# A two-layer graph attention kernel: the turn of the layers with three PSUM tiles for the corrections, gathers chunk by chunk into kept tiles, three row buffers and another order

## The chip, the cores and the metric

The kernel runs on one core of one Trainium2 chip. The core has a matrix engine (PE, with its weight loads listed as PEld), a vector engine (DVE), a scalar engine (ACT), a GpSimd engine (POOL), a sync engine (SP) that issues most plain transfers, and 16 DMA engines. The metric is the device time of one execution in microseconds (us); the median of several runs counts.

## The reference, cut to what matters

A graph has N = 6250 nodes with 256 features and E = 200000 edges, sorted by destination. Two graph attention layers follow each other, the first with 4 heads of 64, the second with 1 head of 256.

```python
h = jnp.maximum(_layernorm(x, axis=-1), 0.0)
x = x + _L0_gnn_ref(h, edge_index, edge_attr_32, ...)

def _gat(x, src, dst, ea, Wg, a_s, a_d, Wge, a_e, b, n, h, f):
    hx = (x @ Wg).reshape(n, h, f)
    he = (ea @ Wge).reshape(-1, h, f)
    al = leaky_relu(einsum(hx, a_s)[src] + einsum(hx, a_d)[dst] + einsum(he, a_e), 0.2)
    m = segment_max(al, dst, num_segments=n)
    al = jnp.exp(al - m[dst])
    al = al / segment_sum(al, dst, num_segments=n)[dst]
    out = segment_sum(hx[src] * al[:, :, None], dst, num_segments=n)
    return out.reshape(n, h * f) + b
...
    te = relu(edge_attr @ We0 + be0) * exp(x @ Wo0 + bo0)[src][:, None]
    s2, d2, ea2 = _add_self_loops(src, dst, te, n)
    x = relu(_gat(x, s2, d2, ea2, Wg0, as0, ad0, Wge0, ae0, bg0, n, HEADS, PH) + x)
    te = relu(edge_attr @ We1 + be1) * exp(x @ Wo1 + bo1)[src][:, None]
    s2, d2, ea2 = _add_self_loops(src, dst, te, n)
    x = _gat(x, s2, d2, ea2, Wg1, as1, ad1, Wge1, ae1, bg1, n, 1, D) + x
    return x + orig
```

Each edge needs the row `hx[src]` of its source node: a gather of about 1 KB per edge. The second layer gathers rows of a table that the first layer makes, so the first layer's last nodes have to be finished before the second layer's gathered rows are all valid. This is the turn of the layers.

## The kernel before

**Tables and steps.** A table T[l] in DRAM holds one row per node for each layer: the features times the layer's weights and a few extra columns. The edges are cut into 1563 chunks of 128, and the chunks into 66 steps per layer: 64 steps of 24 chunks, one of 14, one of 13. Steps are counted through both layers, k = 0 to 131; steps 63, 64 and 65 are the last three of the first layer, step 66 is the first of the second.

**One step.** `gather` (L896 to L907) issues one indirect transfer per chunk from POOL: 128 rows of T[l] into `G[:, c, :]`, a tile of 128 partitions by 24 chunks by 270 columns. Then `logits` (its first reader of the gathered rows is L1158), `ends`, `links` and `maxima` work out the softmax weights with segmented scans on DVE; `scale` (DVE, L1266, first layer) or `scale_rows` (ACT, L1275, second layer) multiplies the rows by them; `onehots` (L1095) builds on DVE a matrix S that says which edge belongs to which of the step's up to 112 nodes; `sums` (L1285) multiplies S by G chunk by chunk on PE and adds up in one PSUM tile `u`; `evict` copies it to SBUF. `finish`, `rows1`, `rows2` and `rows3` turn the sums into node rows: in the first layer `nodes0` ends with two adds into a row buffer (L1370, L1372), `rows1` and `rows2` make the next layer's row on PE (L1378, L439), and `rows3` adds the bias (L443), takes one exponential (L1390) and stores the row to T[1] (L1419) and to a node buffer `nd` (L1421, L1424), all from SP. The edge terms of the next step are made by `rphase1`, `spread`, `parts`, `blocks`, `rphase2`, `adst` and `edge_rows` beside it.

**Buffers.** The G tiles come from three pools of one buffer each, step k from pool k modulo 3. A new tile from a pool can be written only when the tile before it in that pool is done with. `G0` is the tile of step 0, made in the prologue. There are two row buffers `trow1` (L431, L1368), used in turn. Each engine runs its instructions in the order in which the program issues them; nothing is reordered.

**The turn.** `ending` (L770) writes out by hand the order of steps 63 (`a`), 64 (`b`), 65 (`c`) and of step 66 (`after`). Step 66 gathers early, into step 63's tile, chunk by chunk in the order 0 to 23 (`gather(after, a["G"])`), before the last rows of T[1] are there; the last 256 rows of T[1] are filled with zeros beforehand (`lacking`). When the last nodes are done, the missing rows are put in by matrix products: `sources` (L1055) loads the source index of each of step 66's edges, spread over all partitions, into a scratch tile X from pool 2, the tile place of step 65 and later of step 68; `select` (L1063) makes two selector matrices on DVE (L1066), the first in a one-hot buffer, the second in X behind the source row; `lack_rows` (L1068) loads the last 256 rows of T[1] into two tiles; `complete` (L1075) does for each of the 24 chunks two products (L1083) into one of three PSUM regions and an eviction on DVE (L1084) that adds them to G. Two of the three regions are the halves of one PSUM tile `y`. The corrections are issued in three lots of eight with the edge terms of step 66 between them, and its one-hots ahead of the last lot.

After that the main loop goes on with step 66. Each turn of the loop begins with the gather of the next step: step 67's was the first to read the whole of T[1], step 68's goes to a new tile in place of the scratch.

Of the kernel before, what the change touches and what calls it, by code (L numbers as in the profile page):

```python
# [22 lines left out]
F32 = mybir.dt.float32  # L23
BF = mybir.dt.bfloat16
I32 = mybir.dt.int32
# [6 lines left out]
P = 128  # L32
# [47 lines left out]
class Kernel:  # L80
# [329 lines left out]
    def fixed_rows(self):  # L410
        nc, cp = self.nc, self.cp
        self.crow = cp.tile([1, D + self.L[0].H], F32, name="crow")
        self.cl = [cp.tile([36, P + 1], F32, name=f"cl{i}") for i in range(2)]
        for t in self.cl:
            nc.gpsimd.memset(t, -BIG)

        self.cnt = cp.tile([P, self.NS, 2], F32, name="cnt")
        self.mt = cp.tile([P, 4 * C + 4], F32, name="mt")
        x = 33 * C - 1
        fb = cp.tile([P, 8 * C + 2 * x], F32, name="fb2")  # L420
        self.fb = [fb[:, 8 * C * i:8 * C * i + 2 * x] for i in range(2)]
        for t in (self.mt, fb):
            nc.gpsimd.memset(t, 0.0)


        self.aq = [cp.tile([P, 4, 32], BF, name=f"aq{i}") for i in range(2)]
        for t in self.aq:
            nc.gpsimd.memset(t, 0.0)
        self.trow1 = []
        L1 = self.L[1]  # L430
        for i in range(2):  # L431
            self.trow1.append(cp.tile([P, L1.TW + D], F32, name=f"t1row{i}"))
        self.tw4 = cp.tile([P, 4, self.L[0].TW + D], F32, name="tw4")
        self.tws = [self.tw4[:, i, :] for i in range(4)]
# [153 lines left out]
    def index_load(self, g, pool):  # L588
        nc, ss = self.nc, self.groups[g]
        c = self.cs[ss[0]]  # L590
        o = sum(self.cs[:ss[0]])
        w = len(ss) * c
        di = pool.tile([P, 2, 4 * C], I32, name="gi", bufs=2)
        for i, n in enumerate(("dst", "dnx")):
            nc.sync.dma_start(di[:, i, :w], self.a[n][:, o:o + w])
        return di
# [50 lines left out]
    def edges(self, ctx):  # L647
        nc = self.nc
        self.gp += [self.pool(f"gath{i}", 1, ctx) for i in range(1, 3)]
        self.sp = self.pool("onehot", 2, ctx)  # L650
        self.wp = self.pool("work", 2, ctx)
        self.np_ = self.pool("nodes", 2, ctx)
        self.xp = self.pool("index", 1, ctx)
        self.ps_y = self.pool("ps_y", 1, ctx, space=PSUM)
        self.ps_1 = self.pool("ps_1", 1, ctx, space=PSUM)
        self.ps_f = self.pool("ps_f", 1, ctx, space=PSUM)
        self.lf = self.ps_1.tile([P, 512], F32, name="lf")
        nc.vector.memset(self.lf[0:4, 0:1], -BIG)
        steps = self.steps
        self.state = {0: None, 1: None}  # L660
        self.nodes(steps[0])
        self.gather(steps[0])
        if self.NS % 2:
            self.load_lb(1)
        self.spread(steps[0])
        self.parts(steps[0])
        self.blocks(steps[0])
        drain(self.rphase1(steps[0]))
        self.load_ea(1)
        self.rphase2(steps[0])  # L670
        self.adst(steps[0])
        self.onehots(steps[0])
        drain(self.soon)
        self.edge_rows(steps[0])

        pv = late = None
        self.ahead, self.rest = 1, None
        for k, st in enumerate(steps):
            nx = steps[k + 1] if k + 1 < len(steps) else None
            if st["s"] + 2 >= self.NS:  # L680
                continue
            for q in steps[k + 1:k + 3]:
                if q["L"] is st["L"] and "tw" not in q:
                    self.nodes(q)
            self.load_lb(k + 2)
            left = 99
            if self.ahead < len(self.groups):
                left = self.groups[self.ahead][0] - 2 - (self.ahead + 2 >= len(self.groups)) - k
            if self.rest is None and left <= 2:
                gi = self.index_load(self.ahead, self.xp)  # L690
                self.rest = self.index_group(self.ahead, self.xp, gi)
            if st["s"] + 3 == self.NS:
                self.ending(st, *steps[k + 1:k + 3], pv, late, steps[k + 3] if k + 3 < len(steps) else None)
                pv = late = None
                continue
            self.gather(nx)
            st["rows"] = st["L"].l
            drain(self.logits(st))
            self.ends(st)
            self.spread(nx)  # L700
            self.parts(nx)
            y = self.rphase1(nx)
            next(y)
            self.links(st)
            if late:
                self.rows2(late)
            self.load_fl(k + 1)
            self.blocks(nx)
            drain(self.maxima(st))
            drain(y)  # L710
            self.load_ea(k + 2)
            self.rphase2(nx)
            self.adst(nx)
            if "S" not in st:
                self.onehots(st)
            if st["rows"]:
                self.scale_rows(st)
            else:
                drain(self.scale(st))
            self.carried(st)  # L720
            self.sums(st)
            if late:
                self.rows3(late)
                late = None
            self.onehots(nx)
            if pv:
                drain(self.finish(pv))
            self.evict(st)
            if pv:
                self.rows1(pv)  # L730
                late = pv
            self.index_on(left)
            if k == 4 and self.early:
                self.lacking()
            if k >= 6:
                next(self.late, None)
                next(self.late, None)
            self.edge_rows(nx)
            if st["s"] + 4 == self.NS:
                drain(self.finish(st))  # L740
            pv = st
        self.flag()
# [9 lines left out]
    def ending(self, a, b, c, pv, late, after):  # L752
# [41 lines left out]
        self.sums(a, (n // 2, n))  # L794
        early = after and self.early
        if early:
            self.gather(after, a["G"])
        self.load_fl(k + 2)
        drain(self.maxima(b))
        self.evict(a)  # L800
# [59 lines left out]
        drain(f)  # L860
        self.rows1(c)
        self.rows2(c)
        self.rows3(c)
        if after:
            fill = iter(())
            if early:
                self.lack_rows(after)
                self.select(after)
                fill = self.complete(after)
            else:  # L870
                self.gather(after)
            self.nodes(after)
            self.spread(after)
            self.parts(after)
            self.blocks(after)
            for _ in range(C // 3):
                next(fill, None)
            self.rphase2(after)
            self.adst(after)
            for _ in range(C // 3):  # L880
                next(fill, None)
            self.edge_rows(after)
            self.onehots(after)
            drain(fill)

    def flag(self):
        nc = self.nc
# [5 lines left out]
        nc.vector.tensor_reduce(f[:, 0:1], ps[0:1, 0:n], axis=AX.X, op=OP.add)  # L893
        nc.vector.tensor_scalar(self.flag_i, f[:, 0:1], 0.0, None, op0=OP.is_equal)

    def gather(self, st, G=None):  # L896
        nc, L = self.nc, st["L"]
        own = G is not None
        if not own:
            G = self.G0 if st["k"] == 0 else self.gp[st["k"] % 3].tile([P, C, 270], F32, name="G")  # L900
        st["G"] = G
        idx = self.src[:, st["o"]:st["o"] + st["C"]]
        last = st["C"] - 1
        for c in range(0) if st["k"] == 0 and self.CX > last else range(last + 1) if own else (last, *range(last)):
            nc.gpsimd.indirect_dma_start(  # L905
                out=G[:, c, 0:L.TW], out_offset=None, in_=self.T[L.l][0:self.N, :],
                in_offset=bass.IndirectOffsetOnAxis(ap=idx[:, c:c + 1], axis=0))  # L907
# [147 lines left out]
    def sources(self, st):  # L1055

        n = C * P
        X = self.gp[2].tile([P, C, 270], F32, name="G").rearrange("p c d -> p (c d)")
        st["row"] = r = X[:, 0:n].bitcast(I32)
        self.nc.sync.dma_start(r, self.a["srow"].rearrange("c p -> (c p)").partition_broadcast(P))  # L1060
        st["sel"] = [self.sp.tile([P, C, P], F32, name="S").rearrange("p c e -> p (c e)"), X[:, n:2 * n]]

    def select(self, st):  # L1063

        for j, t in enumerate(st["sel"]):
            self.nc.vector.tensor_tensor(t, st["row"], self.k_lack[:, j:j + 1].to_broadcast([P, C * P]), op=OP.is_equal)  # L1066

    def lack_rows(self, st):  # L1068

# [5 lines left out]
    def complete(self, st):  # L1075

        nc, W, G = self.nc, self.L[1].TW, st["G"]
        y = self.ps_y.tile([P, 2, 512], F32, name="y")
        ps = (y[:, 0, :], y[:, 1, :], self.ps_f.tile([P, 512], F32, name="fin"))
        for c in range(C):  # L1080
            q = ps[c % 3][:, :W]
            for j in range(2):
# [255 lines left out]
    def nodes0(self, st, wp, e=None):  # L1338
# [26 lines left out]
        else:  # L1365
            e.tensor_scalar(b, b, 0.0, None, op0=OP.max)
        yield
        st["trow"] = trow = self.trow1[st["s"] % 2]  # L1368
        nrow = trow[:, self.L[1].TW:self.L[1].TW + D]
        e.tensor_add(nrow, xw, hw)  # L1370
        yield
# [178 lines left out]
def drain(g):  # L1550
    for _ in g:
        pass
# [93 lines left out]
```

## Time and profile before

| | |
|---|---|
| median of 3 runs | 4033.51 us |
| lowest and highest | 4033.07 and 4047.03 us |
| the profiled execution | 4041.07 us |
| its span, first to last instruction | 4039.3 us |
| PE busy, share of the span | 2658.8 us, 66% |
| DVE | 2454.5 us, 61% |
| ACT | 1117.3 us, 28% |
| POOL | 2998.3 us, 74% |
| DMA | 585.27 MB, mean 145 GB/s |
| granted PE clock, mean | 0.788 |

The profile is of one execution. A row of a group gives line, engine, operation, output from input, count, then busy time and mean ns of one instruction, then the idle time of the engine just ahead of them and what ended most of it. A row of the waits gives who waited for whom, the total in us, how often, and the longest. A row of a timeline gives start, duration, engine, line, operation, output from input, count, and in brackets the idle time ahead of it with what ended it. A row of the stretches gives the stretch and its length, the busy time of the chosen engine with its count of instructions, the granted PE clock, the DMA share and GB/s. Times in timelines count from the first instruction. Matrix products are pipelined and their ends are modelled. Where an instruction waits for several things, the one named is the last by the profile.

### The profile page before, as it was taken

How to read it: one execution, taken by the hardware profiler on the slowest of the kernel's cores; microseconds unless marked ns; L12 is line 12 of the kernel's file. 1: busy time of each engine (PE TensorE's matmuls, PEld its weight loads, DVE VectorE, ACT ScalarE, POOL GpSimd, SP SyncE). 2: the span in 40 equal slices, each digit the busy share in tenths (PEclk: the TensorE clock that was granted, in tenths of full speed). 3: DMA queues.
4: the chain of work that ended last, by engine and by line, in shares of the span. 5: the costliest groups of instructions: out<-in, count | busy, mean ns of one | idle time of the engine just before them, and what ended most of it. 6: DMA issues, size and time to landing. Idle time of an engine off the chain costs nothing.

```text
span 4039.3 us, 37506 instructions
## 1 busy us (share of the span) xinstructions
PE 2658.8 (66%) x9974; PEld 1744.1 (43%) x9974; DVE 2454.5 (61%) x6096; ACT 1117.3 (28%) x2670; POOL 2998.3 (74%) x3253
## 2 busy tenths in 40 slices
PE   8776676776666676666667656656566566566565
PEld 6444444444444444444444434434334334334343
DVE  7897877877877877877864333344343343343445
ACT  5211111111111111111115434334344344343341
POOL 5777777777777777777757777777777777777775
PEclk9888888888888888888887777777777777777777
DMA  7455555555555555555545455445445445445443
GB/s 245 134 159 145 148 155 147 146 157 143 148 157 146 149 154 144 151 155 142 152 128 151 132 141 142 134 140 140 136 138 143 133 138 144 132 138 143 133 138 97
DMA packets 239747, 585.27 MB, mean 145 GB/s; under 512 B 64315, under 2 KB 96737, under 8 KB 239307
## 3 DMA queue, kind: packets, MB, share of 16 engines
q0 software_dynamic: 150144, 422.75, 39.2%
q1 hardware_dynamic: 88973, 159.40, 12.5%
q8 instruction: 85, 1.39, 0.1%
q14 instruction: 129, 1.06, 0.1%
q10 hardware_dynamic: 416, 0.67, 0.1%
HBM read 544.82 MB, written 38.12 MB: 144 GB/s over the span
## 4 chain that ended last, share of the span: by engine, by line
POOL 32%; DVE 26%; issue 14%; PE 10%; ACT 10%; DMA 8%; DVEq 0%; SPq 0%; ACTq 0%; POOLq 0%
POOL G L905 32%; ACT G L1275 8%; DVE G L1266 7%; DMA G<-T,src 7%; PE y L1005 4%; DVE S L1095 3%; PE u L1285 3%; DVE lb L1029 2%; PE ps L439 1%; DVE m L1214 1%; DVE rt L1144 1%; ACT R L1006 1%; DVE al L1162 1%; DVE al L1160 1%; DVE fb L1175 1%
## 5 line engine op out<-in xcount | busy, mean ns | idle before, releaser
L905 POOL DMA_INDIRECT G<-T,src x3102 | 2946.4, 950 | 989.9 <-issue 912.4
L1285 PE MATMUL u<-G,S 128*128 128x270 f32 (+1 forms) x6252 | 1582.8, 416 | 202.3 <-DVE G L1256 199.0
L1285 PEld LDWEIGHTS u<-G,S 128*128 128x128 f32 x6252 | 1287.4, 207 | 497.0 <-DVE G L1256 225.5
L1275 ACT ACTIVATE G<-G,kw 128x256 f32<-128x256 f32 x1512 | 609.0, 496 | 0.0
L1006 ACT ACTIVATE R<-y,webd 128x1024 f32<-128x1024 f32 (+2 forms) x264 | 235.3, 891 | 1292.9 <-PE y L1005 829.8
L1182 PE MATMUL lf<-ident,fb 128*36 128x128 f32 (+1 forms) x132 | 49.8, 377 | 765.6 <-DVE fb L1175 763.7
L1158 DVE TENSOR_TENSOR G<-rt,G 128x96 f32<-128x96 f32 (+1 forms) x132 | 30.3, 230 | 816.2 <-DMA G<-T,src 815.7
L1266 DVE TENSOR_TENSOR G<-G,kps 128x6144 f32<-128x6144 f32 (+3 forms) x77 | 440.9, 5735 | 0.0
L1095 DVE TENSOR_TENSOR S<-kps,loc 128x3072 f32<-128x3072 f32 x132 | 437.6, 3315 | 4.6
L1005 PE MATMUL y<-ea,webd 64*128 64x256 f32 (+1 forms) x1056 | 386.6, 826 | 49.9 <-ACT R L1006 49.9
L1014 PE MATMUL zad<-R,wea 128*64 128x384 f32 (+1 forms) x1056 | 295.2, 699 | 158.2 <-ACT R L1006 158.2
L1182 PEld LDWEIGHTS lf<-ident,fb 128*36 128x36 f32 (+1 forms) x132 | 15.7, 119 | 806.8 <-DVE fb L1175 804.3
L1014 PEld LDWEIGHTS zad<-R,wea 128*64 128x64 f32 x1056 | 85.2, 182 | 414.3 <-ACT R L1006 334.7
L1290 ACT ACTIVATE U<-u 128x270 f32<-128x270 f32 (+1 forms) x132 | 51.8, 392 | 642.4 <-PE u L1285 642.4
L1317 DVE SCALAR_TENSOR_TENSOR mg<-U,mw 128x1 f32<-128x1 f32 x66 | 14.5, 220 | 281.3 <-ACT mw L1315 281.3
L1005 PEld LDWEIGHTS y<-ea,webd 64*128 64x128 f32 x1056 | 122.7, 284 | 122.7 <-ACT R L1006 68.4
L1248 DVE SCALAR_TENSOR_TENSOR G<-U,kw,G 1x257 f32<-1x257 f32 x62 | 29.6, 478 | 182.6 <-ACT G L1275 182.6
L1116 PE MATMUL zad<-a,Q 128*128 128x12 bf16 (+1 forms) x132 | 26.0, 197 | 157.9 <-DVE a L1111 157.5
L439 PE MATMUL fin<-wg,h1T 128*128 128x260 f32 x264 | 126.5, 629 | 4.3 <-ACT h1T L1380 4.3
L1144 DVE STREAM_TRANSPOSE rt<-zad 128x768 f32<-128x768 f32 (+1 forms) x130 | 126.1, 970 | 4.5 <-PE zad L1130 4.5
L1029 DVE TENSOR_TENSOR lb<-lb,kps 128x1536 bf16<-128x1536 bf16 (+1 forms) x68 | 112.9, 1661 | 0.0
L1390 ACT ACTIVATE t1row<-t1row 128x1 f32<-128x1 f32 x66 | 13.4, 203 | 354.0 <-DVE t1row L443 354.0
(213 smaller groups left out, 2312.1 us busy)
## 6 DMA issues: line engine op xcount, KB each, us to landing
G<-T,src POOLq DMA_INDIRECT x3102, 2.8
ea<-in_ea_dram SPq DMA_DIRECT2D x64, 768.0 KB
lb<-locrow SPq DMA_DIRECT2D x64, 384.0 KB
nd<-t1row SPq DMA_DIRECT2D x66, 225.8 KB
tw<-nd SPq DMA_DIRECT2D x66, 225.8 KB
tw<-T SPq DMA_DIRECT2D x66, 117.2 KB
T<-t1row SPq DMA_DIRECT2D x66, 113.8 KB
tw<-in_x_dram SPq DMA_DIRECT2D x66, 112.0 KB
```

What stands on the lines that cost most here:

```text
L439: self.nc.tensor.matmul(ps[:, :L.MW], hT[:, k, :], self.wg[L.l][:, k, :], start=(k == 0), stop=(k == 1))
L905: nc.gpsimd.indirect_dma_start(out=G[:, c, 0:L.TW], out_offset=None, in_=self.T[L.l][0:self.N, :], in_offset=bass.IndirectOffsetOnAxis(ap= ...
L1005: nc.tensor.matmul(y[:, i, :n], self.webd[l][r, :], ea[r, w], start=True, stop=True)
L1006: nc.scalar.activation(R[:, :, w], y[:, :, :n], AF.Relu, bias=self.be[l])
L1014: nc.tensor.matmul(st["zad"][i * PH:(i + 1) * PH, o], self.wea[l][0], R[:, i, w], start=True, stop=False)
L1029: V.tensor_tensor(lb[:, :, :n], lb[:, :, :n], self.k_part.unsqueeze(2).to_broadcast([P, i, n]), op=OP.is_equal)
L1095: nc.vector.tensor_tensor(st["S"][:, c0:c1, :], self.k_iota.unsqueeze(1).to_broadcast(w), self.loc[:, o + c0:o + c1].unsqueeze(2).to_broad ...
L1144: V.transpose(rv[:, :32 * c].rearrange("p (b n) -> p b n", b=2), z.rearrange("p (b n) -> p b n", b=2)[:, :, :16 * c])
L1182: self.nc.tensor.transpose(self.lf[0:e.shape[1], 1:P + 1], e, self.ident)
L1266: nc.vector.tensor_tensor(v, v, pw[:, c0:c1, :].unsqueeze(3) .to_broadcast([P, c1 - c0, H, L.F]), op=OP.mult)
L1275: self.nc.scalar.activation(v, v, AF.Copy, scale=st["w"][:, c:c + 1])
L1285: nc.tensor.matmul(st["u"][:, :L.W], S[:, i, :], G[:, i, 0:L.W], start=(j == 0), stop=(j == c - 1))
```

## The change

The diff, whole but for context:

```diff
@@ fixed_rows
-        for i in range(2):
+        for i in range(3):
             self.trow1.append(cp.tile([P, L1.TW + D], F32, name=f"t1row{i}"))
@@ index_load
-        di = pool.tile([P, 2, 4 * C], I32, name="gi", bufs=2)
+        di = pool.tile([P, 2, 4 * C], I32, name="gi", bufs=1)
@@ edges
         self.state = {0: None, 1: None}
+        if len(steps) > 3 and steps[3]["L"].l == 0:
+            steps[3]["own"] = self.G0
@@ ending
         if early:
-            self.gather(after, a["G"])
+            after["own"] = self.steps[after["k"] + 3]["own"] = a["G"]
+            self.gather(after)
...
         self.rows1(c)
         self.rows2(c)
+        if early:
+            self.select(after, 0)
         self.rows3(c)
         if after:
             fill = iter(())
             if early:
                 self.lack_rows(after)
-                self.select(after)
+                self.select(after, 1)
                 fill = self.complete(after)
             else:
                 self.gather(after)
             self.nodes(after)
             self.spread(after)
+            for _ in range(C // 3):
+                next(fill, None)
             self.parts(after)
             self.blocks(after)
-            for _ in range(C // 3):
-                next(fill, None)
             self.rphase2(after)
             self.adst(after)
             for _ in range(C // 3):
                 next(fill, None)
             self.edge_rows(after)
-            self.onehots(after)
             drain(fill)
+            if not early:
+                self.onehots(after)
@@ gather
-    def gather(self, st, G=None):
+    def gather(self, st):
         nc, L = self.nc, st["L"]
-        own = G is not None
+        own, G = "own" in st, st.get("own")
@@ sources
-        X = self.gp[2].tile([P, C, 270], F32, name="G").rearrange("p c d -> p (c d)")
+        G = self.steps[st["k"] + 2]["own"] = self.gp[2].tile([P, C, 270], F32, name="G")
+        X = G.rearrange("p c d -> p (c d)")
@@ select
-    def select(self, st):
-        for j, t in enumerate(st["sel"]):
-            self.nc.vector.tensor_tensor(t, st["row"], self.k_lack[:, j:j + 1].to_broadcast([P, C * P]), op=OP.is_equal)
+    def select(self, st, j):
+        self.nc.vector.tensor_tensor(st["sel"][j], st["row"], self.k_lack[:, j:j + 1].to_broadcast([P, C * P]),
+                                     op=OP.is_equal)
@@ complete
-        y = self.ps_y.tile([P, 2, 512], F32, name="y")
-        ps = (y[:, 0, :], y[:, 1, :], self.ps_f.tile([P, 512], F32, name="fin"))
+        ps = (self.ps_y.tile([P, 2, 512], F32, name="y")[:, 0, :], self.ps_f.tile([P, 512], F32, name="fin"),
+              self.ps_1.tile([P, 512], F32, name="u"))
@@ nodes0
-        st["trow"] = trow = self.trow1[st["s"] % 2]
+        st["trow"] = trow = self.trow1[st["s"] % 3]
```

In words:

- There are three row buffers instead of two, and one buffer instead of two for a group of indices.
- A step whose record has `own` gathers into that tile, in the order 0 to 23, instead of into a new tile with the last chunk first. Steps 3 (into `G0`), 66 and 69 (both into step 63's tile) and 68 (into the scratch tile) have it; before, only step 66 did so.
- The corrections use three PSUM tiles: half of `y`, `fin`, and the tile `u` that the sums use.
- The first selector matrix is made ahead of step 65's `rows3`, the second where both were.
- The first eight corrections come ahead of step 66's `parts` and `blocks`, and step 66's one-hots are made in the main loop, behind its `maxima`.

## The prediction

> **What bounds the kernel now.** I read the page's groups first, then what GpSimd (POOL) waited for, then its busy time by 100 us stretches.
>
> ```profile
> span 4039.3 us, 37506 instructions
> L905 POOL DMA_INDIRECT G<-T,src x3102 | 2946.4, 950 | 989.9 <-issue 912.4
> ...
> POOL G L905 <- issue: 912.4, 2993, 1.0
> POOL G L905 <- PE fin L1083: 16.2, 1, 16.2
> ...
> POOL G L905 <- DMA tw<-in_x_dram: 13.9, 1, 13.9
> ...
> POOL G L905 <- DMA T<-t1row: 9.3, 1, 9.3
> ...
> POOL G L905 <- ACT pen L996: 6.4, 2, 6.1
> ...
> 200.00:300.00 100.00, 75.75 (x80) 0.88 0.58 158
> ...
> 2000.00:2100.00 100.00, 68.19 (x72) 0.80 0.53 154
> 2100.00:2200.00 100.00, 64.29 (x68) 0.83 0.43 121
> ```
>
> POOL issues 3102 gathers of 128 rows, 0.950 us each, with 912.4/2993 = 0.305 us of issue between two: 1.25 us per gather, 30.1 us per step of 24, and 3102 x 1.25 = 3.88 ms of the 4.04. It never rests except in four places: 13.9 us before the first, 6.1, 9.3 and 16.2 us. An ordinary 100 us holds 80 gathers (the count behind the x), the two around the turn of the layers 72 and 68. Nothing else counts unless it makes POOL wait. Whether the rest keeps up is shown by what VectorE's first reader of the gathered rows (L1158) waited for, from 300 to 2000 us and from 2180 to 4000 us:
>
> ```profile
>   DMA G<-T,src: 261.4, 54
>   DMA G<-T,src: 546.7, 61
> ```
>
> 4.8 and 9.0 us per step: in both layers the computing waits for gathers, so whatever POOL gains early or at the turn moves all that follows.
>
> **The change, part by part.**
>
> *Step 3 gathers into G0 chunk by chunk.* Now it takes a new tile and waits until step 0's tile is free.
>
> ```profile
> 147.45 0.95 POOL L905 DMA_INDIRECT G<-T,src  x1 [0.30 <-issue]
> 154.53 0.94 POOL L905 DMA_INDIRECT G<-T,src  x1 [6.13 <-ACT pen L996]
> ...
> 140.27 13.49 PE L1285 MATMUL u<-G,S 128*128 128x270 f32 x48 [0.95 <-DVE G L1266]
> 164.95 12.89 PE L1285 MATMUL u<-G,S 128*128 128x270 f32 x48 [3.40 <-DVE G L1256]
> ```
>
> Step 0's sums end at 140.27 + 13.49 = 153.76 and the gather follows (the ACT instruction named merely ended next to it). The sums read a chunk every 13.49/24 = 0.56 us, so by 148.7, when POOL is free, the first 15 chunks are read, and POOL at 1.25 never catches PE. Gain 6.13 - 0.30 = 5.83. Next late: step 4's gather, then due at 154.53 + 24 x 1.25 - 5.83 = 178.7, needs all of step 1's sums, 164.95 + 12.89 = 177.84 plus the lag of 154.53 - 153.76 = 0.77, 178.6: just free. Step 5's comes 30 us later and needs only the 24.7 us more that lie between two steps' sums (164.95 - 140.27): the margin grows. Bounds of this term: 5.83, and 4.8 if step 1's sums end 1 us later. I take 5.8.
>
> *The turn.* POOL, in order: step 66's 24 gathers (already chunk by chunk into step 63's tile), 67's, 68's.
>
> ```profile
> 2025.32 5.74 PE L1285 MATMUL u<-G,S 128*128 128x270 f32 x24
> 2029.46 0.95 POOL L905 DMA_INDIRECT G<-T,src  x1 [0.30 <-PE u L1285]
> ...
> 2069.10 0.94 POOL L905 DMA_INDIRECT G<-T,src  x1 [9.31 <-DMA T<-t1row]
> ...
> 2097.86 0.95 POOL L905 DMA_INDIRECT G<-T,src  x1 [0.30 <-issue]
> 2115.06 0.94 POOL L905 DMA_INDIRECT G<-T,src  x1 [16.25 <-PE fin L1083]
> ```
>
> Step 66's first gather starts while step 63's last sums, on the same tile, run to 2031.06: chunks of one tile are released singly, and 0.30 us before an own gather shows that such waits cost nothing. Step 67 waits for the last of the new table's rows (step 65's store). Step 68 waits until the scratch tile (source row, second selector) is done with, that is, for the last correction.
>
> *The 9.3 us: third row buffer, one selector ahead of the last rows.* Rows of VectorE, ScalarE, PE and SP there:
>
> ```profile
> 2061.43 0.42 ACT L1364 ACTIVATE fb<-fb 128x256 f32<-128x256 f32 x1 [1.26 <-DVE fb L1362]
> 2061.82 0.33 SPq L1419 DMA_DIRECT2D T<-t1row  x1
> ...
> 2062.87 1.79 PE L439 MATMUL fin<-wg,h1T 128*128 128x260 f32 x4 [0.53 <-ACT h1T L1380]
> ...
> 2063.88 0.32 SPq L1419 DMA_DIRECT2D T<-t1row  x1
> ...
> 2064.84 0.42 DVE L1370 TENSOR_TENSOR t1row<-tw,hw 128x256 f32<-128x256 f32 x1 [3.44 <-DMA nd<-t1row]
> ...
> 2065.70 0.42 DVE L443 TENSOR_TENSOR t1row<-fin,bias 128x260 f32<-128x260 f32 x1
> 2066.04 3.35 DVE L1066 TENSOR_TENSOR S<-G,kps 128x3072 f32<-128x3072 int32 x1
> 2066.39 0.32 SPq L1419 DMA_DIRECT2D T<-t1row  x1
> 2068.33 0.84 SPq L1073 DMA_DIRECT2D U<-T  x2
> 2069.30 3.35 DVE L1066 TENSOR_TENSOR G<-G,kps 128x3072 f32<-128x3072 int32 x1
> ...
> GB/s 10 42 187 104 0 146 177 10 114 340 93 389 441 215 461 307 338 461 461 431 258 425 354 395 135 198 115 0 208 125 0 156 177 0 0 0 83 224 294 222
> ```
>
> VectorE waits 3.44 us because step 65's row buffer is step 63's, still being stored. With three buffers its two adds end at about 2062.3 (after the ReLU of 2061.85), the first selector takes 2062.3 to 2065.6, and L443 (PE is done at 2064.66) runs at 2065.6 instead of 2065.70. So the selector fills the hole and the last store, at 2066.39, moves by 0.1 to 0.2 us. SP forbids much more: its first store waits for step 66's gathers to land (2061.82), and a store follows another in at least 2063.88 - 2061.82 = 2.06, so the third could not leave before 2065.94. Gain 0 to 0.45; I take 0.2. Queued behind the selector on VectorE are L443 and with it the store and POOL, so its own input, the source row, must be there at 2062.3. The last row above is DMA rate from 2048 to 2064 us in 0.4 us slices: the 1.5 MB load raises it until slice 24, 2057.6. It has landed. The second selector now ends at 2069.3 instead of 2072.6.
>
> *The 16.25 us: corrections in three PSUM tiles, gathers into the scratch.*
>
> ```profile
> 2075.37 1.22 PE L1083 MATMUL y<-U,S 128*128 128x260 f32 x2
> 2077.49 0.48 DVE L1084 SCALAR_TENSOR_TENSOR G<-G,known,y 128x260 f32<-128x260 f32 x1 [1.77 <-PE y L1083]
> 2078.03 1.24 PE L1083 MATMUL y<-U,S 128*128 128x260 f32 x2 [0.58 <-DVE G L1084]
> ...
> 2085.16 0.60 PE L1083 MATMUL fin<-U,S 128*128 128x260 f32 x2
> 2086.04 0.60 PE L1083 MATMUL y<-U,S 128*128 128x260 f32 x2
> ...
> 2101.16 3.36 DVE L1095 TENSOR_TENSOR S<-kps,loc 128x3072 f32<-128x3072 f32 x1
> 2114.82 0.48 DVE L1084 SCALAR_TENSOR_TENSOR G<-G,known,fin 128x260 f32<-128x260 f32 x1 [0.39 <-PE fin L1083]
> 2125.76 11.87 PE L1285 MATMUL u<-G,S 128*128 128x261 f32 x48
> ```
>
> Now the halves of one tile exclude each other: the second correction waits for the first's eviction, and VectorE's one-hots (3.36) block all evictions once; 24 take 2075.37 to 2115.3. Afterwards they start when the two tail tiles have landed: issue at 2068.33, plus the 2.71 us that passed from the store's issue (2066.39) to the gather it released (2069.10), gives 2071.0, at the latest 2075.4; I take 2071.4. A correction costs PE 2086.04 - 2085.16 = 0.88 at full clock, about twice that at first. Four slow and twenty fast are 7 + 17.6 = 24.6; the node terms between them (parts now behind eight corrections) about 3.5. End: 2099.5, bounds 2096 (all fast) and 2121 (all slow, late start).
>
> Step 68's gathers can then follow step 67's at 2097.86 + 1.25 = 2099.1. In the scratch, chunks 0 to 10 (270 columns each) lie over the source row, read by 2069.3; chunk 11, due at 2112.9, needs the first two corrections, chunk 22, due at 2126.6, all of them. Even the end at 2121 is in time. Gain 16.25 - 0.30 = 15.95. Were the tile released as a whole, the gather would start at about 2099.8: 15.3.
>
> [...]
>
> *What could be late next.* Step 66's one-hots (3.4) move behind its maxima. Its sums start 2125.76 - 2115.3 = 10.5 us after the last correction, and the same work for step 67 stood in that gap, so one of the two now runs beside the sums. Sums of 66 end near 2099.5 + 10.5 + 11.9 = 2121.9, with all 3.4 exposed 2125.3; step 69's gathers are due at 2129.1, chunk by chunk besides. One index buffer instead of two: the next group's load starts only after the last group has been read; 0. Step order, last chunk first or last: 0.
>
> **Sum.** 5.8 + 0.2 + 15.95 = 22.0 us. The profiled execution took 4041.07 us (span 4039.3): 4019.1 for it. It lies 7.6 above the median of 4033.51, which gives 4011.5.
>
> **Rivals.**
> 1. *The corrections keep their old pace and the scratch is released whole.* Then they only start 4.0 earlier and lose 3.4 of one-hots: step 68 starts 7.4 earlier instead of 15.95, the sum is 13.4: 4020.1. For it: one tile's halves did exclude each other. Against: step 66's gathers.
> 2. *The wait at the start moves on to step 4*, whose margin is 0.1 us: POOL then pays back up to 5.8 there; 16.2 remain: 4017.3. Against: VectorE, not POOL, paces step 1's sums.
> 3. *It does not do what it says*: own tiles are released whole in both places and step 68 finds the corrections as late as now; only 0.2 to 3 us remain: 4032.
> 4. *Slower.* The first selector now stands ahead of the last rows; if its source row lands late, each us delays the store, and POOL, by one. It eats the whole gain from a landing 22 us after 2062.3 on, at 2084; at 2090 the time is 4039. Against: the rates, over by 2058.
>
> **How the numbers follow.** The forecast has 0.70, the rivals 0.12, 0.08, 0.04 and 0.03, more gain 0.03. Three runs of the kernel before went from 4033.07 to 4047.03, so up to 14 us may come on top of a low median, and half of that may be missing below: the range is 4005 to 4025, which takes in the 0.45 of the last store below and rivals 1 and 2 above. Half a per cent, about what a measurement of this kernel can tell from no change, is 20.2 us, just under my 22.0. Of the forecast I count 0.82 on the far side, with the greater gain 0.61 faster; slower is rival 4 with a bad draw of runs, 0.03; the rest, 0.36, lies within.
>
> **What would show it.** Right: no POOL wait over 1 us before the last gather but those of 13.9 and about 9 us; step 68's first gather 0.3 us behind step 67's last; the corrections ending near 30 us after step 67's first gather. Wrong: a POOL wait at step 4, at step 68's chunk 11, or at steps 69 to 72; L1066 waiting for the source row; a 9 us wait grown.

## The result, and the profile after

| | before | after |
|---|---|---|
| median (runs) | 4038.14 us (7) | 4021.34 us (7) |
| lowest to highest | 4033.07 to 4047.03 | 4017.56 to 4023.04 |
| the profiled execution | 4041.07 | 4018.75 |
| its span | 4039.3 | 4017.0 |

The ratio is 0.9957, with a 95% interval of 0.9946 to 0.9968: 17.4 us less, between 12.9 and 21.8. The forecast was 22.0 us and 4011.5; the time lies inside its range of 4005 to 4025, and the forecast gain just beyond the interval. The two profiled executions differ by 22.3.

The page's first group and POOL's waits, of the kernel after (its lines are 6 or 7 further down: the gather is L911):

```profile
span 4017.0 us, 37569 instructions
L911 POOL DMA_INDIRECT G<-T,src x3102 | 2947.6, 950 | 966.4 <-issue 903.3
```

```profile
POOL G L911 <- issue: 903.3, 2965, 0.3
...
POOL G L911 <- DMA tw<-in_x_dram: 12.9, 1, 12.9
...
POOL G L911 <- PE u L1292: 9.4, 31, 0.3
POOL G L911 <- DMA T<-t1row: 9.1, 1, 9.1
```

The same 3102 gathers at the same 950 ns; of the four waits two are gone, the one of 6.1 and the one of 16.2. The row with `PE u L1292` has grown from 9 gathers before to 31, since more tiles are now followed chunk by chunk; none of them comes later than the usual 0.3 us. POOL's timeline at the three places:

```profile
145.93 0.98 POOL L911 DMA_INDIRECT G<-T,src  x1 [0.31 <-issue]
147.22 0.94 POOL L911 DMA_INDIRECT G<-T,src  x1 [0.30 <-PE u L1292]
...
2052.19 0.94 POOL L911 DMA_INDIRECT G<-T,src  x1 [0.30 <-issue]
2062.23 0.94 POOL L911 DMA_INDIRECT G<-T,src  x1 [9.09 <-DMA T<-t1row]
...
2090.99 0.94 POOL L911 DMA_INDIRECT G<-T,src  x1 [0.30 <-issue]
2092.24 0.94 POOL L911 DMA_INDIRECT G<-T,src  x1 [0.30 <-issue]
...
2122.30 0.94 POOL L911 DMA_INDIRECT G<-T,src  x1 [0.30 <-DMA G<-T,src]
```

Step 3 starts at 147.22 and steps 68 and 69 at 2092.24 and 2122.30 without a gap. Only the wait for the table's last store is left. Between the first gathers of steps, in the two executions:

| stretch | before | after | difference |
|---|---|---|---|
| start to step 1 | 88.43 | 86.98 | -1.45 |
| step 1 to 3 | 66.10 | 60.24 | -5.86 |
| 3 to 4 | 30.55 | 30.10 | -0.45 |
| 4 to 66 | 1844.38 | 1845.68 | +1.30 |
| 66 to 67 | 39.64 | 39.23 | -0.41 |
| 67 to 68 | 45.96 | 30.01 | -15.95 |
| 68 to 69 | 30.00 | 30.06 | +0.06 |
| 69 to the last gather | 1864.96 | 1864.88 | -0.08 |
| last gather to the end | 29.28 | 29.82 | +0.54 |

The sum is -22.3, and 21.8 of it is the two large terms of the forecast. The rest nearly cancels in this pair: 1.45 and 0.45 less at the start against 1.30 more in the first layer. The timeline of the last rows of the first layer and of the corrections, after:

```profile
2052.78 0.42 ACT L1371 ACTIVATE fb<-fb 128x256 f32<-128x256 f32 x1 [1.26 <-DVE fb L1369]
2053.23 0.43 DVE L1379 TENSOR_TENSOR t1row<-t1row,fb 128x256 f32<-128x256 f32 x1
...
2053.58 3.35 DVE L1072 TENSOR_TENSOR S<-G,kps 128x3072 f32<-128x3072 int32 x1
...
2055.24 0.33 SPq L1426 DMA_DIRECT2D T<-t1row  x1
...
2056.84 0.42 DVE L443 TENSOR_TENSOR t1row<-fin,bias 128x260 f32<-128x260 f32 x1
...
2057.31 0.32 SPq L1426 DMA_DIRECT2D T<-t1row  x1
...
2059.54 0.32 SPq L1426 DMA_DIRECT2D T<-t1row  x1
...
2063.73 1.21 PE L1090 MATMUL y<-U,S 128*128 128x260 f32 x2 [7.15 <-DMA U<-T]
...
2068.19 0.88 PE L1090 MATMUL u<-U,G 128*128 128x260 f32 x2
...
2068.91 0.60 PE L1090 MATMUL y<-U,S 128*128 128x260 f32 x2
...
2090.48 0.60 PE L1090 MATMUL u<-U,G 128*128 128x260 f32 x2
...
2091.12 0.48 DVE L1091 SCALAR_TENSOR_TENSOR G<-G,known,u 128x260 f32<-128x260 f32 x1 [0.39 <-PE u L1090]
...
2100.97 11.67 PE L1292 MATMUL u<-G,S 128*128 128x261 f32 x48
```

VectorE no longer waits ahead of the two adds (3.44 us before), the first selector stands in the hole, and PE makes the corrections without a wait for an eviction, in 27.4 us instead of 39.4. Before, nine such waits took 7.6 us of PE's time; the longest stood behind step 66's one-hots, which VectorE ran from 2101.16 to 2104.52 and only then two evictions, the second, at 2104.82, of products done at 2101.97:

```profile
2104.96 1.23 PE L1083 MATMUL y<-U,S 128*128 128x260 f32 x2 [2.99 <-DVE G L1084]
```

The same 96 products also kept PE busy for 23.9 us instead of 30.1, at a mean granted clock of 0.89 (2062 to 2093 us) instead of 0.81 (2075 to 2116). Step 66's sums run from 2100.97 to 2112.6, ten us before step 69's gathers need the tile.

### The profile page after: what moved, and what is told of

Same layout as the page of the kernel before. It is cut to its first block, busy times and chain, and to the rows that moved or that the text cites. A ratio compares the mean times of both kernels' runs of the same rounds, so it can differ in the third digit from the quotient of the medians.

```text
span 4017.0 us, 37569 instructions
## 1 busy us (share of the span) xinstructions
PE 2648.1 (66%) x9974; PEld 1738.1 (43%) x9974; DVE 2454.8 (61%) x6096; ACT 1117.6 (28%) x2670; POOL 3000.2 (75%) x3253
## 4 chain that ended last, share of the span: by engine, by line
POOL 31%; DVE 27%; issue 14%; PE 10%; ACT 10%; DMA 7%; DVEq 0%; SPq 0%; ACTq 0%; POOLq 0%
POOL G L911 31%; ACT G L1282 8%; DVE G L1273 8%; DMA G<-T,src 7%; PE y L1011 4%; DVE S L1102 3%; PE u L1292 3%; DVE lb L1035 2%; PE ps L439 1%; DVE m L1221 1%; DVE rt L1151 1%; ACT R L1012 1%; DVE al L1169 1%; DVE al L1167 1%; DVE fb L1182 1%
## 5 line engine op out<-in xcount | busy, mean ns | idle before, releaser
L911 POOL DMA_INDIRECT G<-T,src x3102 | 2947.6, 950 | 966.4 <-issue 903.3
L1292 PE MATMUL u<-G,S 128*128 128x270 f32 (+1 forms) x6252 | 1574.2, 415 | 195.6 <-DVE G L1263 192.0
L1292 PEld LDWEIGHTS u<-G,S 128*128 128x128 f32 x6252 | 1280.5, 206 | 487.6 <-DVE G L1263 218.8
L1324 DVE SCALAR_TENSOR_TENSOR mg<-U,mw 128x1 f32<-128x1 f32 x66 | 14.6, 221 | 281.2 <-ACT mw L1322 281.2
```

The lines of the kernel that those rows point to most:

```text
L911: nc.gpsimd.indirect_dma_start(out=G[:, c, 0:L.TW], out_offset=None, in_=self.T[L.l][0:self.N, :], in_offset=bass.IndirectOffsetOnAxis(ap= ...
L1292: nc.tensor.matmul(st["u"][:, :L.W], S[:, i, :], G[:, i, 0:L.W], start=(j == 0), stop=(j == c - 1))
```

## The experiments

The question after the result was why the medians moved by 17 us where the two traces show 22. Then the two parts were tried alone, then the wait that is left, then parts of the turn were undone.

**The same two kernels, profiled twice more each.**

> The kernel before, profiled once more. Question: is the gain of 17 us in the medians, where the two profiled executions differ by 22, smaller because the old waits differ from run to run? Theory A (the waits depend on PE's granted clock while it makes step 0's sums and the corrections): POOL's two waits that the change removed, 6.1 and 16.2 us in the first trace, come out differently, by 2 us or more in sum, and the run's time follows them. Theory B (the rest of the run varies): they stay within 0.5 us, and what differs is POOL's pace or other waits. Theory C (the runs' times vary outside of what the profile shows): span and time go apart.

> As the run before it, one more draw. Theory A: sum of the two waits differs from 22.4 by 2 us or more in one of the two draws and the time goes with it; theory B: the two waits sum to 22 +- 0.5 in both, and the time differs elsewhere.

> The kernel after, profiled once more. Theory A: its spread is small, since the two waits that follow PE's clock are gone: time within 4017 to 4024, POOL's only waits over 1 us the first (12 to 14 us) and the one for the table's last store (9 +- 0.5). Theory B: it varies as much as the kernel before, 14 us, through POOL's pace.

> As the run before it, one more draw: theory A the same two waits within 1 us; theory B a time that differs by several us with the same waits.

| execution | time, us | wait before step 3 | PE clock, 140 to 152 us | wait before step 68 |
|---|---|---|---|---|
| before | 4041.07 | 6.13 | 0.79 | 16.25 |
| before_again1 | 4041.83 | 4.8 | 0.78 | 16.07 |
| before_again2 | 4043.9 | 2.59 | 1.00 | 14.21 |
| after | 4018.75 | none | 1.00 | none |
| after_again1 | 4020.9 | none | 0.91 | none |
| after_again2 | 4018.34 | none | 1.00 | none |

In the third trace of the kernel before the two waits are 5.6 us shorter than in the first. Stretches of PE work, in the first and in the third trace (busy time with its count, then the granted clock), and the gathers that waited in the third:

```profile
140.00:152.00 12.00, 11.73 (x41) 0.79 0.37 101
...
2075.00:2085.00 10.00, 8.50 (x21) 0.56 0.57 154
...
2105.00:2116.00 11.00, 8.63 (x24) 0.73 0.00 0
```

```profile
140.00:152.00 12.00, 11.39 (x52) 1.00 0.45 119
...
2075.00:2085.00 10.00, 8.20 (x24) 0.65 0.54 153
...
2105.00:2116.00 11.00, 7.59 (x27) 0.84 0.04 12
```

```profile
152.59 0.95 POOL L905 DMA_INDIRECT G<-T,src  x1 [2.59 <-ACT pen L996]
...
2113.39 0.94 POOL L905 DMA_INDIRECT G<-T,src  x1 [14.21 <-PE fin L1083]
```

PE got through 52 of its products, step 0's sums among them, in the same 12 us instead of 41, at full clock, and through the corrections in 37.5 us instead of 39.4. So what a wait for PE costs depends on the clock that PE is granted in that stretch, which differs from run to run. That is not all: between the first two traces the sums take the same time (13.49 and 13.46 us), and the wait still falls from 6.13 to 4.8, because POOL started its gathers 1.8 us later (88.43 and 90.22) and the sums ended only 0.5 us later (153.76 and 154.26). Over three traces each, step 1 to step 3 took 64.5 us before and 60.1 after, step 67 to step 68 took 45.2 and 30.0: 4.3 and 15.2, together 19.5. The first trace, from which the forecast was made, had the longest waits of the three. Theory A holds for the waits, but the time did not go with them: the third execution is the slowest of the three before all the same, because POOL's gathers were busy for 2953.0 us in it instead of 2946.4 and the layers took longer by that; theory B's cause is there too. Theory C falls: time and span differ by 1.7 to 1.9 us in all six. In the kernel after, the only waits over 1 us ahead of gathers are the first (12.9, 15.0 and 14.6 us, where 12 to 14 was expected) and the one for the table's last store (9.09, 9.46 and 9.53).

**The start alone.**

```diff
+        steps[3]["own"] = self.G0
         self.nodes(steps[0])
```

(with the change of `gather` that reads `own`)

> The kernel before with one edit: step 3 gathers into step 0's tile, chunk by chunk. Theory (the wait for step 0's sums is hidden whole): POOL goes from the first gather of step 1 to that of step 3 in 60.1 us (66.1, 64.8 and 62.5 in three traces of the kernel before), no wait at step 4, and the turn keeps its waits of 14 to 16 and 9 us; time 2.5 to 6 us less than before, about 4.3, which is the mean of the three draws. Rival (the wait moves on to step 4, whose margin was 0.1 us): a POOL wait of 1 us or more at step 4, time less than 2 us shorter. Rival (tiles are released whole): the wait before step 3 stays.

4035.17 us (10 runs) against 4038.07 for the kernel before (15), a ratio of 0.999 (0.998 to 1.0): the medians differ by 2.9 us, and the interval goes from no gain to 8 us. The times alone don't show a gain; the trace shows that the wait went. POOL's rows, at step 3 and at step 68:

```profile
148.82 0.94 POOL L907 DMA_INDIRECT G<-T,src  x1 [0.30 <-DMA G<-T,src]
150.07 0.95 POOL L907 DMA_INDIRECT G<-T,src  x1 [0.30 <-PE u L1287]
...
2111.65 0.94 POOL L907 DMA_INDIRECT G<-T,src  x1 [15.36 <-PE fin L1085]
```

The wait is gone although step 0's sums took 13.42 us here and ended at 153.80, after step 3's first gather. So the tile is released chunk by chunk. Step 4 follows after 30.16 us, so the wait did not move on, and the turn keeps its wait.

**The turn alone.**

```diff
-        if len(steps) > 3 and steps[3]["L"].l == 0:
-            steps[3]["own"] = self.G0
```

> The kernel after without the edit at step 3. Theory: POOL's wait of 2.5 to 6 us before step 3 is back, step 68's gathers follow step 67's after 30.0 us (46.0, 45.8 and 44.0 before), and the time is 14 to 16 us under that of before, 4 us over that of after. If the two parts did not add up, this and the run with the start alone would not sum to about 19.5 us.

4023.78 us (6 runs), 0.9966 (0.9953 to 0.9979): 13.7 us less, between 8 and 19. Step 3 waits again, step 68 does not:

```profile
152.08 0.94 POOL L909 DMA_INDIRECT G<-T,src  x1 [4.01 <-ACT pen L1000]
...
2094.80 0.95 POOL L909 DMA_INDIRECT G<-T,src  x1 [0.30 <-issue]
```

That is as expected, but for the time over that of after, 2.4 us in the medians instead of 4. The two parts add up: 0.10% and 0.34% alone, 0.43% together, each with an interval of about 0.1% either way.

**The wait that is left: the three table stores ahead of the node stores.**

```diff
-        self.rows3(c)
+        self.rows3(c, 1)          # bias, exponential, store to T[1]
+            for q in (a, b, c):
+                self.rows3(q, 2)  # stores to the node buffers
```

(and the same for steps 63 and 64)

> The kernel after, with the three stores of the new table's last rows (steps 63, 64, 65) issued by SP ahead of their six smaller stores to the node buffers, which follow in one lot. Theory (the 9 us wait before step 67 is bound by SP's order, 2.06 us from a table store to the next, and only then by the last row's exponential): the last table store leaves 0.2 us after the exponential instead of 2.0 us later, the wait falls from 9.1 or 9.5 to about 7.2, the time by 2 us to about 4018. Rival (bound by the computing of step 65's row): the wait stays at 9 us. Rival (moved cost): the wait falls, but step 66's terms, which read the node buffers, are late, and the corrections' second lot starts later by up to 2 us; that costs nothing unless step 69 waits.

The time is 4019.78 us (5 runs), 0.9957 (0.9942 to 0.9972), as after. The wait stayed. POOL's row, the three table stores, and what SP waited for between 2045 and 2075 us:

```profile
2067.16 0.94 POOL L913 DMA_INDIRECT G<-T,src  x1 [9.28 <-DMA T<-t1row]
```

```profile
2059.91 4.59 SPq L1429 DMA_DIRECT2D T<-t1row  x3
```

```profile
SPq L1429 <- DMA G<-T,src: 10.5, 3, 7.2
...
SPq L1429 <- DMA T<-t1row: 3.2, 2, 1.7
SPq L1433 <- DMA nd<-t1row: 3.2, 2, 1.8
```

None of the three expectations named the cause. With nothing between them on SP, the second and third table stores still waited, 3.2 us in two waits, for the table store ahead of them to land. The first left at 2059.91 and the third 4.27 us later, where it was 4.30 in the kernel after. The computing of step 65's row did not hold it: the exponential ended at 2062.94, 1.2 us before the last store left. In the kernel after, no such wait is listed between 2040 and 2068 us, only these two of SP ahead of its stores of rows, beside the waits for gathers:

```profile
SPq L1428 <- DMA nd<-t1row: 0.4, 2, 0.2
SPq L1426 <- ACT t1row L1397: 0.2, 1, 0.2
```

There SP's own node stores fill the time between two table stores. So two limits of nearly the same length stand one behind the other, SP's order and the landing of the store before, and taking away the first alone gains nothing. All three stores go to one table; why each waits for the one before, no run showed. The chain is: step 66's gathers land, then three stores one after the other, each some 2 us, then the gather.

The same run shows something about the turn that it was not made for. The two tail tiles were now loaded only at 2072.01, behind the six node stores that follow the last table store, so the corrections started 8.6 us after step 67's first gather, instead of 1.5, and ended 36.8 us after it, instead of 29.4:

```profile
2097.22 0.95 POOL L913 DMA_INDIRECT G<-T,src  x1 [0.30 <-issue]
...
2102.82 0.60 PE L1092 MATMUL u<-U,G 128*128 128x260 f32 x2
```

Step 68's gathers start at 2097.22, 30.06 us after step 67's, while products that read the second selector in the scratch run to 2103.4. No gather of steps 68 and 69 waits. Had the scratch been released whole, POOL would have stood for some 6 us there, an estimate from these two rows. So there was a moved cost, as the third expectation had it, but by another way and larger, and the gathers into the scratch hid it.

**Parts of the turn undone.** Four kernels were to tell the three PSUM tiles, the gathers into the scratch and the third row buffer apart, one of them twice.

```diff
 halves:         ps = (y[:, 0, :], y[:, 1, :], fin)     # instead of y, fin, u
 scratch_whole:  step 68 takes a new tile               # no "own" for it
 halves_whole:   both
 two_rows:       self.trow1[st["s"] % 2]                # instead of 3
```

> The kernel after with the corrections in the halves of one PSUM tile and a third tile, as before. Theory (the gathers into the scratch, chunk by chunk, hide the corrections whatever their pace): the corrections take some 8 us longer, to about 36 us after step 67's first gather, and POOL still goes from step 67 to step 68 in 30.0 us and on to step 69 in 30.0; time as after. Rival (the three tiles carry the gain): a POOL wait at step 68, at chunk 11 or later, or at step 69.

> The kernel after with a new tile for step 68, so that the scratch is released whole, and three PSUM tiles. Theory (the corrections end 1.2 us before step 68's gathers are due): wait 0 to 1 us at step 68, time as after within 1 us. Rival (the gathers into the scratch carry the gain): a wait of several us at step 68.

> Both undone: corrections in halves, scratch released whole; the order of the corrections, the selectors and the one-hots as after. Theory (either edit alone removes the wait, and only without both does it come back): POOL waits 5 to 9 us before step 68 (16.2, 16.1, 14.2 before), the rest of the 15 us being the earlier start and the one-hots moved out. Rival (order does nothing): 14 to 16 us. Rival (order does it all): under 1 us.

> The kernel after with two row buffers, the first selector still ahead of the last rows. Theory: VectorE waits 3.4 us or more for the store of step 63's row to the node buffer, then makes the selector, and the last table store leaves 3.4 us later: POOL's wait before step 67 is 12.5 instead of 9.1 to 9.5. Rival (the third buffer is worth nothing, SP's order sets the store): the wait stays within 0.5 us.

> As halves_whole (corrections in the halves of one PSUM tile and a third, scratch released whole, the new order kept), on a chip where the kernel before takes its usual 4033 to 4047 us. Theory: the corrections take some 8 us more than the 27 of the kernel after and end about 37 us after step 67's first gather, so POOL waits 5 to 9 us before step 68 (14.2 to 16.2 before); time 5 to 9 us over that of after, 4025 to 4030. From the same trace: with the scratch released chunk by chunk, chunk 11 would be due 43.8 us and chunk 22 57.5 us after step 67's first gather; if the corrections end before 43.8, the halves would have cost nothing there. Rival (the order does nothing, the two edits do it all): a wait of 14 to 16 us. Rival (the order does it all): under 1 us.

These five executions met two chips on which the kernel before itself takes 4904 us (one run) and 4800.71 us (13 runs). In the five traces from there PE pauses again and again for a reason that no semaphore shows (1141.6 to 1232.1 us ahead of its sums with no releaser but "issue"), and the mean granted clock is 0.72 to 0.73, where the other traces have 0.78 to 0.79. What PE's sums waited for, in two_rows and then in the kernel after on its chip:

```profile
PE u L1292 <- issue: 1196.9, 615, 3.7
```

```profile
L1292 PE MATMUL u<-G,S 128*128 128x270 f32 (+1 forms) x6252 | 1574.2, 415 | 195.6 <-DVE G L1263 192.0
```

There POOL is busy for 61 or 62% of the span and waits for PE some 130 times, so the times say nothing on the questions asked (one run each: halves 4914.47, scratch_whole 4890.02, halves_whole 4895.18, two_rows 4897.76; ten runs of halves_whole_b 4811.12, a ratio of 1.0023, 1.0011 to 1.0035, to the kernel before). The expectations in numbers, all for the usual chip, are not tested; two_rows is lost altogether, since its wait for the table store was 42.4 us and that of scratch_whole, with three buffers, 40.7. How the scratch is released can be read from the waits at step 68, in scratch_whole and then in two_rows, which has all of the turn but the third buffer:

```profile
2513.44 0.95 POOL L911 DMA_INDIRECT G<-T,src  x1 [0.30 <-issue]
2533.60 0.94 POOL L911 DMA_INDIRECT G<-T,src  x1 [19.21 <-PE u L1090]
```

```profile
2541.65 0.95 POOL L911 DMA_INDIRECT G<-T,src  x1 [0.30 <-issue]
2548.52 0.95 POOL L911 DMA_INDIRECT G<-T,src  x1 [5.92 <-remote]
2550.70 0.95 POOL L911 DMA_INDIRECT G<-T,src  x1 [1.23 <-remote]
2552.93 0.95 POOL L911 DMA_INDIRECT G<-T,src  x1 [1.29 <-PE fin L1090]
```

Released whole, step 68's first gather stands until the last correction (19.21 us; 23.47 in halves_whole). Released in pieces, fifteen of its gathers go out while the corrections still run (to 2561.7), and seven later ones are held singly, for 5.92 us and then 0.8 to 1.7 each; where the profile names the releaser, it is a correction (`remote` is a releaser that it can't place). So the scratch is followed chunk by chunk. On that chip this gained little further on: from step 67's first gather to step 69's it was 77.1 us in two_rows and 79.0 in scratch_whole, but 85.4 in halves and 83.3 in halves_whole. The two kernels that differ in the PSUM tiles alone, scratch_whole and halves_whole, took 47.2 and 51.5 us for the corrections; that is one run each.

## Why the prediction was right, and what was off

- *What bounds the kernel*: POOL's 1.25 us per gather, and only its four waits to be had. Held: pace and count are unchanged, the two waits that went are the gain.
- *Step 3, 5.8 us*: mechanism as forecast, no wait at step 4 (rival 2 falls, by the run of the start alone). In the profiled pair 5.86. As a mean of three traces 4.3, below the term's own bounds of 4.8 and 5.83: it was mis-sized, because the one trace with the longest wait was taken for every run.
- *Third row buffer and selector, 0.2 us*: the adds followed at once, the selector filled the hole, the source row was there (rival 4 falls: no wait ahead of L1072). In the profiled pair the last store left 4.57 us after the first before and 4.30 after, so 0.27. Over three traces nothing is left of it: POOL's wait before step 67 was 9.31, 9.56 and 9.29 before, 9.09, 9.46 and 9.53 after. The bound, a table store at most every 2.06 us by SP's order, held; what the forecast did not see is the second limit of the same length behind it, the landing of the store before. What the third buffer alone is worth on the usual chip was not settled.
- *The turn, 15.95 us*: in the profiled pair exactly that, as a mean of three 15.2, for the same reason as at the start. The corrections ended 29.4 us after step 67's first gather; the forecast's 2099.5 was 30.4. My four slow corrections, an estimate from the trace of the kernel before, where four were slow (2075.37 to 2083.60), missed a little in this trace: PE turned fast between 4.5 and 5.2 us after the first correction (2068.19 and 2068.91 against 2063.73), after two and a half. Over the five traces of this order on the usual chip it was 3.6 to 6.2 us, each time less than the 7 us of the estimate.
- *Which edit of the turn carries it*: in the trace after, the last product that reads the scratch ends at 2091.08 and step 68 is due at 2092.24, so a release as a whole would just have done there; that is read from the trace and not shown by a run. There the shorter corrections are enough. With the corrections 7 us later, in the run with the stores first, the release in pieces kept step 68 from waiting. How much of the shortening is due to the three PSUM tiles and how much to the other order stays open.
- *Rivals 1 and 3* fall with step 68's gather at 30.01 us after step 67's, rival 3 also with step 3's, which started before step 0's sums had ended (147.22 against 149.61).
- *What could be late next*: nothing was. Step 66's sums ended at 2112.6, where the forecast had 2121.9 to 2125.3 less the 6.9 us of the earlier gains.
- *The size of the whole*: 22.0 forecast, 17.4 measured, just outside its interval, which ends at 21.8. The three traces account for 19.5; the rest is within the interval. The time itself was missed by 9.8 us: 5.2 because the medians differ by 16.8 instead of 22.0, and 4.6 because the median of three runs came out at 4033.51 where seven give 4038.14. That the first pair comes so close, at 22.3, is luck in part: the later two pairs give 20.3 and 16.5 at the two waits, the first 21.8.
- *The chances*: the forecast gave 0.61 to a gain of more than half a per cent. Measured are 0.43%, so the less likely outcome came. Half a per cent is 20.2 us, and the two waits were worth 19.5 in the mean.
- *The spread*: the first seven runs of the kernel before spread over 14 us, those after over 5.5. That the two waits which followed PE's clock made part of it fits the traces, but is not shown: fifteen later runs of the kernel before spread over 7.9 us, and five with the stores first, without the two waits, over 9.0.

## What to carry to other kernels

Where one queue sets the pace at a constant rate, list its waits first; here the two that other engines' work could cover were worth nearly their full length (19.5 of 20.0 us in the mean of three traces), and the two gains added up within the noise. Profile the kernel more than once before pricing a wait: one that ends with an engine whose clock differs from run to run has no single length (6.13, 4.8 and 2.59 us here), and a median of three runs is a reference to be checked too. Before an order of transfers is changed, look at what the second of two equal transfers would wait for if the order were gone: here it was the landing of the first, 3.2 us in two waits, and nothing was gained (4019.78 us against 4021.34).

## What the runs showed of the hardware that was not expected

- The same 48 products of step 0's sums took 13.49, 13.46 and 11.21 us in three executions of one program, at granted clocks of 0.79, 0.78 and 1.00 in that stretch. In the first traces of both kernels the corrections start at a granted clock of 0.50 (2075.3 to 2076.4 us before, 2063.7 to 2064.5 after); their first fast product came 3.6 to 6.2 us after their first one in five traces of the new order, and 6.3 to 8.8 in four of the old, where PE also waits for evictions.
- On two of the chips the same program takes 4904 and 4800.71 us instead of 4038. In two_rows PE stood for 1196.9 us ahead of its sums with no releaser but "issue" (615 times, up to 3.7 us), in halves_whole_b on the other chip for 1141.6 (621 times, up to 4.1), at the same counts and bytes. POOL is not the bound there, and the kernel after with two of its parts undone gained nothing over the kernel before (1.0023, 1.0011 to 1.0035). Why PE pauses there stays open.
- Three stores to one table at places known at run time left SP about 2 us apart with other stores between them (2055.24, 2057.31, 2059.54) and, where nothing stood between them, still took 4.3 us from the first to the third, because SP waited for the one before to land.
